# One summed tile for two: the weight sums of two heads over tile pairs in three attention blocks

## The chip, the core and the metric

The kernel runs on one core of one Trainium2 chip. The metric is device microseconds of one execution. The kernel before was run three times; each execution of it does the whole computation in one launch.

## What is computed

A graph attention layer over 4096 nodes of 256 features and 4 heads, and after it a mixture of 8 experts of which each node uses two.

```python
e = leaky_relu(s_row[:, :, None] + s_col[:, None, :], negative_slope=0.2)   # per head, 4096 x 4096
e = where(adj > 0, e, -9e15)
att = softmax(e, axis=-1)
out = einsum('hij,hjk->hik', att, h)          # then elu, + residual, layer norm, + x
...
top_w, top_i = top_k(xf @ Wg + bg, 2)          # softmax over the two
out = sum over e of w_dense[:, e] * (gelu(xf @ W1[e] + b1[e]) @ W2[e] + b2[e])
```

The softmax is not formed as such. For a neighbour `j` and a node `i` of one head the kernel holds a weight without the factor that belongs to `j` alone; that factor, exp(0.2 s_col), is multiplied into the features `ha` and stands by itself in `unit`. The sum over all `j` of weight times features goes to `acc`, and the sum over all `j` of weight times factor goes to `den`; the quotient of the two is the head's output.

## The kernel before

**Blocks and tiles.** The 4096 nodes `i` are cut into four blocks of 1024 (`a`, 0 to 3; the words block 1 to 4 are used for them). A block runs over 32 tiles `j` of 128 neighbours each. A tile has 128 neighbours on the partitions and 1024 nodes along the row, and each node row stands in two halves of 512. `attend` and `weigh` do one tile.

**One tile.** SyncE loads the adjacency of the tile. ScalarE turns it into a bfloat16 mask `am` of zeros and twos (`mask_of`, L1603; three buffers). VectorE makes one weight tile `w` of 128x1024 float32 for each of the four heads in the order 1, 0, 2, 3, each with one scalar_tensor_tensor: the maximum of the row term `er` and the neighbour's `eb`, and the minimum of that and the mask (L1686). The `w` tiles have ten buffers, two and a half tiles' worth, and this is how far VectorE can run ahead of TensorE. TensorE then multiplies: for each head and half two 128x32 matmuls into `acc` (`rows_of_head`, L1195) and one 128x2 matmul into `den` (`weights_of_head`, L1204). [...]A float32 matmul shows as two records in the trace, so a tile has 32 records of `acc` and 16 of `den`.

**The end of a block.** `finish_blocks(a)` is a generator. Its first step, taken when the block ends, copies `den` and `acc` to SBUF on ScalarE, so that the next block can use the banks. The other steps are taken one by one while the next block runs, one after each tile, by `next(pending, None)` in the tile loop. Step 1 turns `den` and forms its reciprocals (`shares_of`), steps 1 to 17 make the block's output rows (results, elu, residual, two layer norms, with three DMAs that add or store), steps 18 to 25 route the rows to experts (`route_rows`: transposes `ptx`, logits, top two, and at step 25 the ranks by the matmul `pk`, L1322 and L1324). Step 26 turns the ranks to places `at` (L1342), and 16 indirect DMAs on GpSimd's queue scatter the rows to the expert lists in DRAM (L1382).

**Order.** The order of TensorE's instructions is written out by hand inside the attention: `queue` and `order_of` chain every matmul and transpose in the order of the program text. The other engines are ordered by a planner at build time, which takes, of the instructions that it holds ready, the one that stands first in the text. Every engine then works its own list strictly in order. DMAs are issued from SyncE's, ScalarE's and GpSimd's lists.

**Behind the attention.** The expert phase works through jobs of 256 rows. `up` is the first product (L1867), `down` the second (L1901). The rows of job 1 on are loaded by `load_full` (L560, the tile `early`) after the attention, `ROOM` of them ahead of the first job. Within TensorE's written order `up` of job 0 comes first, then pieces of the last block's end, then the transposes of job 1's rows (`turn_rows_of`, L604), then `down` of job 0. The program keeps every read of the expert lists behind the scatters that stand before it in the text: the first `early` load waits for the semaphores of all 16 scatters of block 3. Jobs 0 to 8 (`EARLY` is 9) hold rows of the first two blocks alone; their places were planned in block 4.

[...]four for `acc`, one for `den`, and three that the helper `bank` gives out in turn.

Of the kernel before, what the change touches and what calls it, by code (L numbers as in the profile page):

```python
# [10 lines left out]
F32 = mybir.dt.float32  # L11
I32 = mybir.dt.int32
BF16 = mybir.dt.bfloat16
AF = mybir.ActivationFunctionType
OP = mybir.AluOpType
# [17 lines left out]
FINAL = (16, 15, 15, 15, 13, 13, 12, 9)  # L33
LIST = 36 * CH
PLACE = (2, 3, 0, 1)
ORDER = (1, 0, 2, 3)


# [6 lines left out]
def gat_then_moe(  # L45
# [34 lines left out]
    MID = BOTH - EARLY  # L80
    LATE = 2 * N // TT - BOTH
    SURE = 2
    ROOM = 10
    KT = -(-N // TT)
    LAG = 6

# [132 lines left out]
    def forward(apart, stack):  # L219
# [392 lines left out]
        with ExitStack() as layer:  # L612
# [588 lines left out]
            def weights_of_head(w, j, half, h):  # L1201
# [4 lines left out]
                    start=(j == 0 and half == 0), stop=(j == NT - 1 and half == HB - 1),  # L1206
                ))

            def attend(w, j, halves, sums_first=None):


                def first_heads():
                    for half in halves:
                        for h in (1, 0):
                            rows_of_head(w, j, half, h)

                def other_heads():
                    for half in halves:
                        for h in (1, 0):
                            weights_of_head(w, j, half, h)  # L1220
                        rows_of_head(w, j, half, 2)
                    for half in halves:
                        rows_of_head(w, j, half, 3)
                        for h in (3, 2):
                            weights_of_head(w, j, half, h)

                parts = (first_heads, other_heads)
                if sums_first is None:
                    sums_first = j in (0, NT - 1)
                for add in reversed(parts) if sums_first else parts:  # L1230
                    add()

            def shares_of(pd):

                z = small.tile([P, TB, H, HB], F32, tag="z", name="z")
                for h in range(0, H, 2):
                    nc.vector.reciprocal(z[:, :, h : h + 2], pd[:, :, PLACE[h] : PLACE[h] + 2, :HB])
                return z
# [151 lines left out]
            def finish_blocks(a):  # L1390
# [12 lines left out]
                for t in range(TB):  # L1403
                    order_of(nc.tensor.transpose(
                        pd[:, t].rearrange("p h q -> p (h q)"), ud[:, ts(t, P)], ident
                    ))
                z = shares_of(pd)
                xe = rows_listed()
                n = HB * TB
                halves = [(half, slice(half * TB, (half + 1) * TB)) for half in range(HB)]  # L1410
# [108 lines left out]
            def turn_sums(ud):  # L1519
                pd = bank([P, TB, H, Q], "pd")  # L1520
                for t in range(TB):
                    queue(nc.tensor.transpose(
                        pd[:, t].rearrange("p h q -> p (h q)"), ud[:, ts(t, P)], ident
                    ))
                z = shares_of(pd)
                return z

            def last_block(b, u, z, given, xe):

# [64 lines left out]
            def load_mask(a, j):  # L1594

                at = load_adj(gat, range(a * R, (a + 1) * R), j, 1, 3)
                am = gat.tile([P, R], BF16, tag="am", name="am", bufs=3)
                with tc.issue_after(marks["eb"]):
                    mask_of(at[:, 0], am)
                return am  # L1600
# [75 lines left out]
            else:  # L1676

                with tc.tile_pool(name="sep", bufs=2) as work:

                    def weigh(er, am, j, halves):  # L1680
# [10 lines left out]
                                w[half][h] = wh[:, half]  # L1691
                        return w

                    both = list(range(HB))
                    ers = [er0, er1]
                    er = er0
# [27 lines left out]
                        if j == 0:  # L1724
                            sums_turned(row)
                    for a in range(NR):
                        later = None
                        for j in range(0 if a else TB, NT):
                            attend(
                                weigh(er, load_mask(a, j), j, both), j, both,  # L1730
                                False if (a, j) == (NR - 1, NT - 1) else None,
                            )
                            if a == 0:
                                prepare_at(TB + j)
                            if pending:
                                next(pending, None)
                            if a == 1 and j == 1:
                                turn_biases()
                            if a + 1 == NR and j == 3:
# [366 lines left out]
```

## Time and profile before

| | us |
|---|---|
| median of three runs | 1264.79 |
| the three runs | 1264.42, 1264.79, 1270.94 |
| the profiled execution | 1259.9 |
| its span, first to last instruction | 1258.2 |
| busy in it: TensorE matmul, VectorE, ScalarE, GpSimd | 1243.7, 842.8, 451.6, 240.2 |
| mean granted TensorE clock | 0.997 |

The attention fills the first 778 us of the span and the expert phase the rest. On TensorE block 2 runs from 255.9 to 432.5 us, block 3 to 604.3 and block 4 to 778.3. Busy time is the time in which an engine had an instruction in work; what is said of waits comes from the semaphores. A line number in the profile is that of the listing above.

### The profile page before, as it was taken

The page shows a single profiled execution, that of the slowest core. Times are in us where ns is not written, and L with a number is a line of the kernel's source. Part 1 is how long each engine was busy: PE and PEld are TensorE (multiplying, and loading weights), DVE is VectorE, ACT ScalarE, POOL GpSimd, SP SyncE. Part 2 cuts the span into 40 slices and gives each one's busy share as a digit, 9 for nine tenths or more (in the row PEclk, how much of TensorE's full clock was granted, in tenths as well). Part 3 has the DMA queues.
Part 4 walks back from the last instruction along what each step waited for, and adds up shares of the span by engine and source line. Part 5 has one row for each costly group of instructions (what it writes and reads, how often), then busy time and mean ns, then how long its engine had stood idle before and what let it go on. Part 6 is the DMA issues. An engine that isn't in the chain of part 4 may idle for free.

```text
span 1258.2 us, 22490 instructions
## 1 busy us (share of the span) xinstructions
PE 1243.7 (99%) x8916; PEld 650.9 (52%) x8916; DVE 842.8 (67%) x1566; ACT 451.6 (36%) x929; POOL 240.2 (19%) x217
## 2 busy tenths in 40 slices
PE   9999999999999999999999999999999999999997
PEld 5444444332232332332325324888888876666686
DVE  7998887879999989999999996845111121111120
ACT  4332322255522375322655322533333332222322
POOL 4000000001002601006110024135222322122222
PEclk9999999999999999999999999999999999999999
DMA  6333433436533656335366423967777795454662
GB/s 215 118 119 124 158 105 102 166 102 133 187 105 104 231 118 201 103 100 158 112 167 194 119 80 108 329 184 225 234 208 222 207 210 115 102 139 105 139 156 42
DMA packets 131603, 190.22 MB, mean 151 GB/s; under 512 B 45560, under 2 KB 101744, under 8 KB 131104
## 3 DMA queue, kind: packets, MB, share of 16 engines
q1 hardware_dynamic: 109456, 145.39, 38.7%
q0 software_dynamic: 20544, 36.74, 13.2%
q10 hardware_dynamic: 1488, 6.55, 1.4%
q8 instruction: 72, 1.18, 0.4%
q14 instruction: 43, 0.35, 0.1%
HBM read 155.77 MB, written 29.74 MB: 147 GB/s over the span
## 4 chain that ended last, share of the span: by engine, by line
PE 94%; DVE 3%; issue 1%; DMA 1%; ACT 1%; POOLq 0%; SPq 0%; DVEq 0%; ACTq 0%
PE acc L1195 33%; PE po L1901 18%; PE ph L1867 17%; PE den L1204 17%; PE pr L1050 2%; DVE w L1686 2%; PE ph L1098 2%; PE pt L604 1%; PE ptx L1250 0%; DMA early<-lists 0%; PE acc L891 0%; PE pt L777 0%; PE ptr L1488 0%; PE po L1940 0%; PE pl L1261 0%
## 5 line engine op out<-in xcount | busy, mean ns | idle before, releaser
L1195 PE MATMUL acc<-w,ha 128*32 128x512 f32 x4096 | 671.6, 595 | 1.3 <-ACT u L1398 0.9
L1686 DVE SCALAR_TENSOR_TENSOR w<-er,eb,am 128x1024 f32<-128x1024 f32 x496 | 606.1, 1277 | 32.1 <-PE den L1204 31.8
L1204 PE MATMUL den<-w,unit 128*2 128x512 f32 x2048 | 467.8, 593 | 0.1
L1195 PEld LDWEIGHTS acc<-w,ha 128*32 128x32 f32 x4096 | 184.7, 110 | 294.3 <-issue 255.5
L1603 ACT ACTIVATE am<-adj 128x1024 bf16<-128x1024 int32 x124 | 130.6, 1054 | 348.8 <-DVE w L1686 208.9
L1867 PE MATMUL ph<-xT,w 128*128 128x256 f32 (+5 forms) x864 | 229.9, 423 | 0.2 <-ACT hT L1871 0.2
L1901 PE MATMUL po<-w,hT 128*128 128x256 f32 (+1 forms) x1040 | 229.7, 379 | 0.0
L1871 ACT ACTIVATE hT<-ph,bias 128x256 f32<-128x256 f32 (+5 forms) x216 | 111.3, 517 | 289.7 <-PE ph L1867 175.4
L1901 PEld LDWEIGHTS po<-w,hT 128*128 128x128 f32 (+1 forms) x1040 | 194.8, 189 | 30.7 <-issue 3.4
L1867 PEld LDWEIGHTS ph<-xT,w 128*128 128x128 f32 x864 | 163.4, 190 | 59.7 <-issue 38.0
L1204 PEld LDWEIGHTS den<-w,unit 128*2 128x2 f32 x2048 | 93.7, 85 | 148.2 <-issue 139.8
L1926 POOL DMA_INDIRECT out<-o,ids x66 | 102.0, 1546 | 323.7 <-DMA out<-o,ids 126.9
L1914 DVE SCALAR_TENSOR_TENSOR o<-po,share,b2s 128x256 f32<-128x256 f32 (+2 forms) x66 | 31.8, 483 | 196.4 <-PE po L1901 188.3
L1382 POOL DMA_INDIRECT lists<-xe,at x64 | 88.1, 1377 | 267.3 <-issue 184.3
L608 DVE COPY xT<-pt 128x256 f32<-128x256 f32 x12 | 5.1, 424 | 62.0 <-PE pt L604 54.1
L1851 DVE STREAM_TRANSPOSE xT<-xr 128x960 f32<-128x960 f32 (+5 forms) x10 | 10.0, 1004 | 31.6 <-PE ph L1867 31.1
L1050 PE MATMUL pr<-wr,xT 128*128 128x256 f32 x128 | 30.4, 381 | 0.2 <-ACT er L1144 0.2
L1889 ACT ACTIVATE b2s<-b2b,share 128x256 f32<-128x256 f32 x68 | 30.3, 503 | 0.0
L1438 POOL DMA_DIRECT2D xf<-in_x x6 | 8.1, 1351 | 105.4 <-ACT xf L1437 105.4
L1118 POOL DMA_DIRECT2D residual<-rb x6 | 4.7, 784 | 121.2 <-DVE rb L1065 121.2
L1050 PEld LDWEIGHTS pr<-wr,xT 128*128 128x128 f32 x128 | 24.1, 190 | 5.4 <-issue 0.9
L1098 PE MATMUL ph<-wall,xT 128*128 128x264 f32 x96 | 24.6, 399 | 0.0
(391 smaller groups left out, 658.5 us busy)
## 6 DMA issues: line engine op xcount, KB each, us to landing
adj<-in_adj SPq DMA_DIRECT2D x126, 512.0 KB
w<-in_L_ffn_W SPq DMA_DIRECT2D x54, 1024.0 KB
er<-parts ACTq DMA_DIRECT2D x3, 2048.0 KB
early<-lists SPq DMA_DIRECT2D x16, 260.0 KB
lists<-zeros POOLq DMA_DIRECT2D x8, 520.0 KB
residual<-rb POOLq DMA_DIRECT2D x8, 512.0 KB
rb<-residual SPq DMA_DIRECT2D x8, 512.0 KB
out<-y POOLq DMA_DIRECT2D x8, 512.0 KB
```

Of the source, the lines that this page charges most:

```text
L1050: order_of(nc.tensor.matmul(pr[:, k, :], turned[b][:, c, ts(t0 + k, P)], wr[:, c, :], start=(c == 0), stop=(c == DC - 1),))
L1098: order_of(nc.tensor.matmul(phs[t - t0], xT[:, c, ts(t, P)], wall[:, c, :], start=(c == 0), stop=(c == DC - 1),))
L1195: queue(nc.tensor.matmul(acc[half][h // 2][here : here + Q, :], ha[:, j, h * K + g * Q : h * K + (g + 1) * Q], w[half][h], start=(j == 0), ...
L1204: queue(nc.tensor.matmul(den[here : here + HB, :], unit[:, j, h, 1 - half : 1 - half + HB], w[half][h], start=(j == 0 and half == 0), stop ...
L1382: ins = nc.gpsimd.indirect_dma_start(lists, bass.IndirectOffsetOnAxis(ap=at[:, k, t : t + 1], axis=0), xe[:, t, :], None,).ins
L1603: nc.scalar.activation(am, at, AF.Relu, scale=2.0)
L1686: marks["w"] = nc.vector.scalar_tensor_tensor(wh[:, these], er[:, these, h], eb[:, j, h : h + 1], mask[:, these], op0=OP.max, op1=OP.min,).ins
L1867: order_of(nc.tensor.matmul(ph, job["w1"][:, c, ts(f, P)], xT[:, c, :], start=(c == 0), stop=(c == DC - 1),))
L1871: job["gelu"] = nc.scalar.activation(hT[:, f, :], ph, AF.Gelu, bias=job["bias"][:, f : f + 1]).ins
L1901: order_of(nc.tensor.matmul(po[:size], hT[:, f, k * CH : k * CH + size], w2[:, f, :], start=(f == 0), stop=(f == FC - 1),))
L1914: given_out.append(nc.vector.scalar_tensor_tensor(o[:size], po[:size], share[:size, k : k + 1], b2s[k][:size], op0=OP.mult, op1=OP.add,).ins)
L1926: added.append(add().ins)
```

## The change

In blocks 2 to 4 (`a` of 1 to 3) the tile loop takes other helpers.

- In the first 18 tiles (`PAIRED`) the mask is copied once more by ScalarE, as 512 words of 32 bits, into one of two PSUM banks (`packed_mask`), and VectorE's four instructions read it there. The banks are two of the three that `bank` gives out.
- For heads 1 and 0 these tiles go to `den` in pairs. When the second tile of a pair is weighed, ScalarE multiplies the first tile's weights by the quotient of the two tiles' factors (`ratio`, made once in block 2) into a slot of the `er` tile that is idle, GpSimd adds the second tile's weights in place (`added_pair`), and the next tile's `attend_both` multiplies the sum with the second tile's factors. So heads 1 and 0 have one set of `den` matmuls per pair in place of two; heads 2 and 3 and all `acc` matmuls stay. The rows of `den` get another order (`place_of`), which `shares_of` follows.
- The steps of `finish_blocks` are no more taken from the block's first tile on, one per tile: they are taken from tile 18 on, two per tile, and up to nine after the last tile.
- `ROOM`, the number of row tiles loaded ahead in the expert phase, goes from 10 to `EARLY - 1`, which is 8.

```diff
+PAIRED = 18
+ADDED = (1, 0)
...
-    ROOM = 10
+    ROOM = EARLY - 1
...
+            def attend_both(w, j, alone, summed=None, sums_first=False):
+                halves = range(HB)
+                def first_heads():
+                    for half in halves:
+                        for h in (1, 0):
+                            rows_of_head(w, j, half, h)
+                def other_heads():
+                    if summed:
+                        for h in ADDED:
+                            for half in halves:
+                                weights_by_half(summed, j - 1, half, h)
+                    if alone:
+                        for h in (1, 0):
+                            for half in halves:
+                                weights_by_half(w, j, half, h, start=(j == 0))
+                    for half in halves:
+                        for h in (2, 3):
+                            rows_of_head(w, j, half, h)
+                    for h in (2, 3):
+                        for half in halves:
+                            weights_by_half(
+                                w, j, half, h, start=(j == 0 and not alone), stop=(j == NT - 1)
+                            )
+                parts = (first_heads, other_heads)
+                for add in reversed(parts) if sums_first else parts:
+                    add()
...
+                    def packed_mask(am, j):
+                        pm = masks[j % 2]
+                        nc.scalar.copy(pm.bitcast(I32), am.bitcast(I32))
+                        return pm.bitcast(BF16)
...
+                    def added_pair(idle, j):
...
+                        for k, h in enumerate(ADDED):
+                            s = slots[:, 2 * (j // 2 % 2) + k]
+                            nc.scalar.activation(
+                                s, made[0][h], AF.Copy, scale=ratio[:, j // 2, h : h + 1]
+                            )
+                            nc.gpsimd.tensor_tensor(s, s, made[1][h], OP.add)
...
                         for j in range(0 if a else TB, NT):
-                            attend(
-                                weigh(er, load_mask(a, j), j, both), j, both,
-                                False if (a, j) == (NR - 1, NT - 1) else None,
-                            )
+                            if a == 0:
+                                attend(weigh(er, load_mask(a, j), j, both), j, both)
+                            else:
+                                w = weigh_both(er, a, j)
+                                attend_both(
+                                    w, j, j >= PAIRED, summed,
+                                    j == 0 or j == NT - 1 and a + 1 < NR,
+                                )
+                                summed = None
+                                if j < PAIRED and j % 2:
+                                    summed = added_pair(ers[(a + 1) % 2], j)
...
-                            if pending:
-                                next(pending, None)
+                            if pending and j >= PAIRED:
+                                for _ in range(2 if j + 1 < NT else 9):
+                                    next(pending, None)
```

## The prediction

> **What bounds the kernel now.** I read the engines' busy time, the costliest groups, the chain that ended last, the busy time by block, and the timelines of VectorE, GpSimd and SyncE about the block ends.
>
> ```profile
> PE 1243.7 (99%) x8916; PEld 650.9 (52%) x8916; DVE 842.8 (67%) x1566; ACT 451.6 (36%) x929; POOL 240.2 (19%) x217
> ...
> L1686 DVE SCALAR_TENSOR_TENSOR w<-er,eb,am 128x1024 f32<-128x1024 f32 x496 | 606.1, 1277 | 32.1 <-PE den L1204 31.8
> ```
>
> TensorE is busy in 99% of the span. VectorE's 32 us before its weights end on TensorE: its buffers were full. The chain, at the end of the attention, gives the price of a record, and the timeline of VectorE that of a weight instruction:
>
> ```profile
> 773.48 1.72 PE acc L1195 x16
> ```
> ```profile
> 403.35 6.06 DVE L1686 SCALAR_TENSOR_TENSOR w<-er,eb,am 128x1024 f32<-128x1024 f32 x5
> ```
>
> Sixteen records take 1.72 us, 107.5 ns each, so a tile's 48 take 5.16. Five weights take 6.06, the last 1.28 long, so they start 1.195 apart: 4.78 a tile. VectorE gains 0.38 us a tile, which pays for the rest of its work. By block:
>
> ```profile
> 255.90:432.50 176.60, 175.68 (x1635) 53.84 (x1638) 167.26 (x198) 75.52 (x153) 33.14 (x22) 0.99 0.47 137
> 432.50:604.30 171.80, 171.80 (x1623) 52.81 (x1619) 166.09 (x190) 74.06 (x151) 29.75 (x23) 1.00 0.49 142
> 604.30:778.30 174.00, 173.59 (x1623) 61.62 (x1615) 161.26 (x215) 70.91 (x149) 27.62 (x22) 1.00 0.43 124
> ```
>
> After the length come TensorE, weight loads, VectorE, ScalarE, GpSimd. VectorE stands at 94% of TensorE: a gain on TensorE beyond some 6 us a block would meet it.
>
> GpSimd does little, but late in block 4 this (64 scatters in all, starts 1.3 to 2.4 us apart):
>
> ```profile
> 746.94 1.28 POOL L1382 DMA_INDIRECT lists<-xe,at  x1 [81.76 <-DVE at L1342]
> 748.53 2.09 POOL L1382 DMA_INDIRECT lists<-xe,at  x1 [0.30 <-issue]
> ...
> 770.89 0.97 POOL L1382 DMA_INDIRECT lists<-xe,at  x1 [0.30 <-issue]
> 772.17 0.97 POOL L1382 DMA_INDIRECT lists<-xe,at  x1 [0.30 <-issue]
> ```
>
> They end 5 us before the attention does. Behind it the chain goes through the rows of job 1, and TensorE's timeline shows what they hold up:
>
> ```profile
> 780.59 5.91 DMA early<-lists
> ...
> 788.71 6.91 PE po L1901 x32
> ```
> ```profile
> 778.56 7.17 PE L1867 MATMUL ph<-xT,w 128*128 128x256 f32 x32
> ...
> 787.53 0.41 PE L604 MATMUL pt<-ident,early 128*128 128x128 f32 x2 [0.48 <-PE ptr L1536]
> ...
> 788.55 7.07 PE L1901 MATMUL po<-w,hT 128*128 128x256 f32 x32
> ```
>
> The load is issued 2.3 us after the last attention matmul (778.3) and lands 5.9 us later; the transposes of its rows (`pt`) wait, and `po` of job 0 comes behind them in TensorE's order.
>
> [...]a scatter, which reads its places in SBUF, takes 0.97 us after VectorE's last weight at 768.4 and often 2.0 to 2.1 before. [...]
>
> **The change, part by part.**
>
> *Matmuls.* A pair saves two heads times two halves, 8 records: 0.86 us. 9 pairs in 3 blocks: 27 x 0.86 = **-23.2**. All of it is on TensorE's path.
>
> *Masks in PSUM.* 18 x 4 x 3 = 216 weights read one input there. At 1.195 a paired tile takes VectorE 4.78, TensorE (18 x 5.16 - 7.7)/18 = 4.73: VectorE loses 0.9 us in 18 tiles, which its lead covers (9 us at block starts, from the starts of `w` and of the matmuls on them in the timeline). The price in PSUM is not shown for this form. [...]the 512-wide product from PSUM (L1539) takes 0.69 us, and the 1024-wide one in SBUF (L1446) 1.22, which less half of the weight form's width (1.278 - 0.743 = 0.535) is also 0.69. Nothing excludes a few ns less, but TensorE would cap that gain. I take **0**[...].
>
> *ScalarE.* A pair adds two mask copies and two scaled copies. [...]hidden by ScalarE's idle time, **0**. Without that cover the copy is late for the weight two tiles on.
>
> *GpSimd.* [...]The sum is wanted one tile after the second weight: **0** in the steady state. An add that takes 4.7 us or more would set the pace.
>
> *Steps at double pace.* VectorE's share of the first ten steps costs 12 us over its 4.78 a tile (block 3: tiles 2 to 9 took 50 us in the timeline). In five tiles in place of eight its lead falls from 9.5 by 12, and gets back 1.9 from the tiles and 2.7 from the transposes (tiles 0 and 1 of block 3 took 6.72 and 6.31 us): about 2 us stay. In block 4 before, a lead of 2 cost TensorE 0.9 us. DMAs of a step have half the time too: the accumulating one goes out at 306.3 and is waited for until 312.1, against 7.7 us for three steps. I take 1 a block, **+3**, ends 0 and +9. Block 4's early plan no longer meets these steps: **-1**.
>
> *Scatters at the block's end.* Step 25, the rank matmul, moves from tile 24 to tile 30, and TensorE's order keeps it behind that tile: 5.2 us before the block's end E. From it to the first scatter were 5.6 us (741.36 to 746.94). So 16 scatters start at about E+0.4, and all stand in GpSimd's list before the next block's adds if the planner holds them ready first, as I expect, since VectorE's lead is then some 4.5 us and the adds want the weights of tile 1. [...]they take 0.97 + 0.30: 20.3 us[...]. TensorE wants that sum in tile 2: two tiles of 4.3 and 1.7 of the third, E+10.3. It stands for 15 us, with VectorE behind it on full buffers. This meets blocks 3 and 4: **+30**. If the adds of the first pair come ahead, the second pair's are late: [...]8 each. Bounds 0 (finely mixed) and 17 each.
>
> *The load after block 4.* Its scatters, now at E-2 to E+0.6, take 20[...] to 26 us (as before): they end at E+18 to E+27[...]. The first `early` load waits for all of them, and SyncE's list stands behind it with job 1's weights. It was issued at E+2.3. TensorE has `up` of job 0 (7 us) and then the transposes of these rows, ahead of `down`. So everything after moves by 18 to 27 us; I take **+20**, lower end 15. `ROOM` moves loads 9 and 10 behind: these waited on the same scatters; **0**.
>
> Sum: -23.2 + 0 + 3 - 1 + 30 + 20 = **+28.8**. The profiled execution has 1259.9 us (1.7 outside its span of 1258.2) and would have 1289; it is 4.9 below the median of the runs, 1264.79, from which I forecast **1292 us**.
>
> **Rivals.**
> 1. *The adds come ahead of the scatters*: 8 in place of 15 a block, +15: 1280. For it: VectorE can lead by two tiles; against it: the steps eat that lead just before.
> 2. *Scatters and adds mix well, so only the late load is lost*: 0 to 3 a block, the load 20 to 27: -1 to +12, 1264 to 1277. [...]against it: all 16 become ready at one moment.
> 3. *Faster*: the scatters reach neither TensorE nor the load, because the route steps run early enough: -23 + 3 - 1, 1244; it decides if the last scatter lands before E+7 and the adds before E+10. Against it: the rank matmul is fixed behind tile 30, and 16 x 1.27 us follow.
> 4. *GpSimd locks VectorE out although the masks are in PSUM*: each add would hold a weight back[...]. Against it: [...]the scatters' spread.
> That the pairing does not take place at all I exclude: the matmuls are issued by number.
>
> **How the numbers follow.** The forecast 0.45, rival 1 0.22, rival 2 0.12, faster 0.13, the lock or another slow case 0.08. The runs tell about 0.5%, 6 us, from no change. Forecast and rival 1 are slower (0.67), with 4 and the upper half of rival 2 (0.02) 0.77; rival 2 leaves 0.10 to same; faster 0.13. The forecast's own range is 1280 to 1311 (waits of 12 to 17 us, load 15 to 27, steps 0 to 9: +15 to +46). With rivals 1 and 2 the range is 1260 to 1311, which leaves out rivals 3 and 4.
>
> **What would show it.** The `den` group at 1832 records in place of 2048; weights near 1.28 us with PSUM masks; [...]scatters beginning within 2 us of the ends of blocks 2, 3 and 4; a TensorE wait on GpSimd of 10 to 15 us early in blocks 3 and 4; the first `early` load issued some 20 us behind the attention. Wrong would be: block 2 not shorter than 172 us (matmul price), no wait on GpSimd (order), or `po` of job 0 within 12 us of the attention's end (load).

## The result, and the profile after

The changed kernel takes 1360.82 us (median of four runs, 1358.88 to 1361.47), the kernel before beside it 1265.17: a ratio of 1.0745, with a 95% interval of 1.0723 to 1.0766. The forecast was 1292, the range 1260 to 1311. The direction is right; the size, 95.7 us, is 3.3 times the predicted 28.8, and outside the range. The profiled execution took 1360.74 us, with a span of 1359.0, 100.8 more than that of before.

From the page of the changed kernel, the engines' busy time and the groups that answer to those shown of before (out and in, shape, count, then busy us, mean ns of one, idle us before it and its releaser):

```profile
PE 1260.4 (93%) x8700; PEld 657.4 (48%) x8700; DVE 857.8 (63%) x1570; ACT 538.7 (40%) x1037; POOL 344.1 (25%) x271
...
L1756 DVE SCALAR_TENSOR_TENSOR w<-er,eb,pm 128x1024 f32<-128x1024 f32 x216 | 259.4, 1272 | 16.3 <-POOL er L1775 11.3
...
L1756 DVE SCALAR_TENSOR_TENSOR w<-er,eb,am 128x1024 f32<-128x1024 f32 x168 | 210.4, 1294 | 41.4 <-PE den L1217 40.6
...
L1775 POOL TENSOR_TENSOR er<-er,w 128x1024 f32<-128x1024 f32 x54 | 127.4, 2382 | 143.6 <-DVE w L1756 127.4
...
L1300 PE MATMUL ptx<-ident,xe 128*128 128x128 f32 x64 | 13.6, 341 | 39.9 <-ACT xe L1528 39.7
```

TensorE was busy in 99% of the span and is now in 93% of a longer one: it does 216 records less and stands for some 99 us. VectorE's weights are no dearer with the mask in PSUM (1272 ns against 1294), and the adds take 2.38 us. New is the last line. These 64 transposes of the rows to be routed, which TensorE had never waited for, are waited for 39.7 us. The same group in the costliest groups of the kernel before:

```profile
L1250 PE MATMUL ptx<-ident,xe 128*128 128x128 f32 x64 | 8.6, 278 | 0.0
```

The prices of a record and of a weight are as before. In the changed kernel's chain of work that ended last, and in its timeline of VectorE:

```profile
481.04 3.00 PE acc L1197 x28
```
```profile
289.30 23.91 DVE L1756 SCALAR_TENSOR_TENSOR w<-er,eb,pm 128x1024 f32<-128x1024 f32 x20
```

28 records take 3.00 us, 107.1 ns each, and twenty weights, the last 1.27 long, start 1.19 us apart. The busy time by stretch, block 2, 3, 4 and what lies behind (start and end, length; then TensorE, weight loads, VectorE, ScalarE, GpSimd; then the granted clock, DMA share and GB/s):

```profile
260.10:457.40 197.30, 174.79 (x1562) 52.91 (x1562) 170.56 (x198) 105.71 (x190) 56.28 (x32) 0.92 0.42 123
457.40:652.10 194.70, 175.39 (x1543) 60.55 (x1545) 167.95 (x190) 101.20 (x184) 56.77 (x33) 0.94 0.43 128
652.10:860.90 208.80, 182.33 (x1552) 58.38 (x1547) 176.73 (x220) 97.77 (x182) 66.71 (x43) 0.93 0.36 104
860.90:1359.00 498.10, 474.81 (x2102) 375.43 (x2102) 124.30 (x547) 154.31 (x319) 142.84 (x109) 0.98 0.67 172
```

Blocks 2 to 4 took 176.6, 171.7 and 174.4 us before and take 197.3, 194.7 and 208.7. Block 2 begins 4.2 us later, and what lies behind the attention has grown from 479.6 to 498.1. So 78 us are in the blocks, 4 at the start of block 2 and 18.5 behind the attention.

To see where in a block, I took from the trace the start of each tile's first record on TensorE, and from the length of the tile its records at 107.4 ns (48 in a whole tile, 40, 48 or 56 in a paired or adjoining one). What is left, called the surplus of a tile below, is TensorE's other work and its waits, in us for blocks 2 to 4 together:

| tiles | 0-2 | 3-17 | 18-19 | 20-25 | 26-27 | 28-31 | sum |
|---|---|---|---|---|---|---|---|
| before | 12.1 | 4.9 | 6.1 | 2.8 | 1.0 | 0.9 | 27.8 |
| after | 28.3 | 8.9 | 21.8 | -0.1 | 59.5 | 10.6 | 129.0 |
| difference | +16.2 | +4.0 | +15.7 | -2.9 | +58.5 | +9.7 | +101.2 |

With the records saved (-23.2), the start of block 2 (+4.2) and the part behind (+18.5) that is 100.7, the whole of the 100.8. Of it 81 lie in tiles 18 to 31, where the moved steps are, and where no tile is paired. Of the 81, some 48 us are waits of TensorE for two sets of transposes that belong to these steps: 8.4 at `ptr` (steps 1 and 2, tile 18) and 39.7 at `ptx` (step 18, tile 26).

**Tile 26.** From the timeline of all engines about it in block 2 (start, duration, what; in brackets the idle time before, and its releaser):

```profile
396.85 1.22 DVE L1496 TENSOR_TENSOR y<-y,gam 128x1024 f32<-128x1024 f32 x1
...
398.37 0.85 POOL L1497 DMA_DIRECT2D y<-xf  x1 [1.45 <-DVE y L1496]
...
405.52 0.42 ACT L1503 ACTIVATE m<-y 128x256 f32<-128x256 f32 x1 [1.18 <-DMA y<-xf]
...
407.25 0.17 DVE L217 TENSOR_SCALAR off<-total 128x8 f32<-128x8 f32 x1 [3.20 <-ACT m L1503]
407.33 4.87 DVE L1756 SCALAR_TENSOR_TENSOR w<-er,eb,am 128x1024 f32<-128x1024 f32 x4
407.46 0.51 ACT L209 ACTIVATE m<-y,off 128x256 f32<-128x256 f32 x1 [0.24 <-DVE off L217]
...
414.73 1.28 DVE L1756 SCALAR_TENSOR_TENSOR w<-er,eb,am 128x1024 f32<-128x1024 f32 x1
...
416.32 0.17 DVE L1515 TENSOR_TENSOR off<-off,r 128x8 f32<-128x8 f32 x1
416.52 1.09 ACT L1528 ACTIVATE xe<-y,off,r 128x256 f32<-128x256 f32 x2 [1.96 <-DVE off L1515]
417.17 0.18 PEld L1300 LDWEIGHTS ptx<-ident,xe 128*128 128x128 f32 x1 [13.54 <-ACT xe L1528]
417.17 0.48 PE L1300 MATMUL ptx<-ident,xe 128*128 128x128 f32 x1 [12.61 <-ACT xe L1528]
```

This is one chain through four engines and a transfer: VectorE's product, GpSimd's accumulating transfer (7.2 us to landing), ScalarE's sums, VectorE's mean, ScalarE's squares, VectorE's roots, ScalarE's normalised rows, TensorE's transposes. From the product to the transposes it takes 20 us. But these are only the last of the steps, and the four tiles between their places in the text, 20.6 us, would just do; the product itself came late, in TensorE's tile 25, though it stands behind tile 22 in the text. What shows the stand is the whole chain between two of TensorE's own instructions, from the last `ptr` transposes to the first `ptx`. From TensorE's timeline of the changed kernel, and from the timelines of TensorE and ScalarE of the kernel before, in block 2:

```profile
360.59 1.12 PE L1538 MATMUL ptr<-ident,u 128*128 128x128 f32 x4 [0.55 <-ACT y L1543]
```
```profile
271.56 1.09 PE L1488 MATMUL ptr<-ident,u 128*128 128x128 f32 x8
...
337.85 4.04 ACT L1478 ACTIVATE xe<-y,off,r 128x256 f32<-128x256 f32 x8 [1.96 <-DVE off L1465]
...
355.32 1.09 PE L1250 MATMUL ptx<-ident,xe 128*128 128x128 f32 x8
```

Before, the first rows `xe` came 65 us behind the end of `ptr`, and TensorE, at one step a tile, reached `ptx` only after 83: it never waited. At two steps a tile only eight tiles stand between the two, 41 us of records, while the chain takes 55 (361.7 to 417.2). TensorE takes its list in order, and stands for most of the difference, 12.6 us.

TensorE doesn't wait for weights there; three of the next tile's four were made when it stopped. VectorE, though, is not far ahead and not at rest. It waits 3.2 us for ScalarE's sums, and makes seven more weights during the stand, three of them between the instructions of the roots. So its own weights are part of the chain's length.

This stand of TensorE, 12.6 us without work, costs more than its length. The same stretch by busy time, clock in the third column from the end:

```profile
404.60:409.00 4.40, 0.00 (x0) 0.00 (x0) 1.75 (x3) 3.25 (x15) 0.77 (x1) 1.00 0.95 300
409.00:417.10 8.10, 0.00 (x0) 0.00 (x0) 7.41 (x12) 5.18 (x16) 0.00 (x0) 0.51 0.75 250
417.10:421.00 3.90, 3.78 (x16) 1.88 (x20) 0.00 (x0) 3.90 (x10) 0.00 (x0) 0.50 0.22 84
421.00:424.00 3.00, 3.00 (x24) 0.64 (x20) 0.00 (x0) 0.51 (x2) 0.00 (x0) 0.70 0.00 0
```

TensorE's granted clock is 1.00 in the first 4.4 us of standing, 0.51 in the other 8.1, and still half for some 5.7 us after it has begun again (0.50 in the first 3.9, and by the mean of 0.70 some 1.8 of the last 3.0). Its first eight transposes take 2.80 us there, where the eight of tile 27 take 1.09, and the 16 records behind them 3.33, where the next 16 take 1.89: 3.2 us beside the 12.6. Tile 26 has 15.5 us beyond its records and tile 27 some 4.

**Behind the attention.** TensorE's and SyncE's timelines answer to the last lines shown of before:

```profile
868.21 1.13 PE L1971 MATMUL ph<-xT,w 128*128 128x256 f32 x4 [3.02 <-issue]
875.29 2.07 PE L1971 MATMUL ph<-xT,w 128*128 128x256 f32 x4 [5.96 <-issue]
880.97 3.78 PE L1971 MATMUL ph<-xT,w 128*128 128x256 f32 x8 [3.60 <-ACT hT L1975]
...
887.06 0.63 PE L606 MATMUL pt<-ident,early 128*128 128x128 f32 x4
887.52 7.07 PE L2005 MATMUL po<-w,hT 128*128 128x256 f32 x32
```
```profile
862.63 0.70 SPq L1897 DMA_DIRECT2D w<-in_L_ffn_W  x1
879.04 0.37 SPq L562 DMA_DIRECT2D early<-lists  x1
```

The first `early` load goes out 18.2 us behind the attention's end at 860.9, in place of some 2, as forecast. But TensorE doesn't stand at the transposes of its rows: it stands in `up` of job 0, between its own matmuls, while the scatters run (857.6 to 877.6), and at 887 the transposes don't wait. Two waits lie one under the other there, and the profile can't say what either would cost alone.

### The profile page after: what moved, and what is told of

It reads as the page before. It is cut to its first block, busy times and chain, and to the rows that moved or that the text cites. A ratio compares the mean times of both kernels' runs of the same rounds, so it can differ in the third digit from the quotient of the medians.

```text
span 1359.0 us, 22410 instructions
## 1 busy us (share of the span) xinstructions
PE 1260.4 (93%) x8700; PEld 657.4 (48%) x8700; DVE 857.8 (63%) x1570; ACT 538.7 (40%) x1037; POOL 344.1 (25%) x271
## 4 chain that ended last, share of the span: by engine, by line
PE 72%; DVE 11%; issue 9%; DMA 2%; ACT 2%; POOL 2%; another core or an unknown queue 1%; POOLq 0%; DVEq 0%; ACTq 0%
PE acc L1197 22%; PE po L2005 17%; PE ph L1971 16%; DVE w L1756 9%; PE den L1217 5%; PE den L1206 4%; PE pr L1052 2%; PE ph L1100 2%; DMA y<-xf 2%; POOL lists L1432 1%; PE ptx L1300 1%; POOL er L1775 1%; PE pt L606 1%; PE acc L893 0%
## 5 line engine op out<-in xcount | busy, mean ns | idle before, releaser
L1197 PE MATMUL acc<-w,ha 128*32 128x512 f32 x4096 | 585.1, 609 | 19.0 <-DVE w L1756 12.5
L1197 PEld LDWEIGHTS acc<-w,ha 128*32 128x32 f32 x4096 | 162.8, 112 | 323.3 <-issue 283.4
L1756 DVE SCALAR_TENSOR_TENSOR w<-er,eb,pm 128x1024 f32<-128x1024 f32 x216 | 259.4, 1272 | 16.3 <-POOL er L1775 11.3
L1971 PE MATMUL ph<-xT,w 128*128 128x256 f32 (+5 forms) x864 | 234.2, 428 | 14.4 <-issue 10.6
L1756 DVE SCALAR_TENSOR_TENSOR w<-er,eb,am 128x1024 f32<-128x1024 f32 x168 | 210.4, 1294 | 41.4 <-PE den L1217 40.6
L1217 PE MATMUL den<-w,unit 128*2 128x512 f32 x1104 | 173.0, 597 | 3.0 <-issue 2.8
L1775 POOL TENSOR_TENSOR er<-er,w 128x1024 f32<-128x1024 f32 x54 | 127.4, 2382 | 143.6 <-DVE w L1756 127.4
L1735 DVE SCALAR_TENSOR_TENSOR w<-er,eb,am 128x1024 f32<-128x1024 f32 x112 | 138.2, 1276 | 13.3 <-PE den L1206 13.3
L1206 PE MATMUL den<-w,unit 128*2 128x512 f32 x512 | 117.6, 592 | 0.1
L1432 POOL DMA_INDIRECT lists<-xe,at x64 | 62.5, 976 | 144.4 <-issue 58.7
L1746 ACT COPY pm<-am 128x512 int32<-128x512 int32 x54 | 31.8, 591 | 119.3 <-DVE w L1756 113.6
L1217 PEld LDWEIGHTS den<-w,unit 128*2 128x2 f32 x1104 | 35.2, 86 | 88.9 <-issue 87.7
L1772 ACT ACTIVATE er<-w,ratio 128x1024 f32<-128x1024 f32 x54 | 59.1, 1137 | 5.7 <-DVE lesse L289 3.0
L1300 PE MATMUL ptx<-ident,xe 128*128 128x128 f32 x64 | 13.6, 341 | 39.9 <-ACT xe L1528 39.7
```

The costliest lines, as they stand in the source:

```text
L1197: queue(nc.tensor.matmul(acc[half][h // 2][here : here + Q, :], ha[:, j, h * K + g * Q : h * K + (g + 1) * Q], w[half][h], start=(j == 0), ...
L1206: queue(nc.tensor.matmul(den[here : here + HB, :], unit[:, j, h, 1 - half : 1 - half + HB], w[half][h], start=(j == 0 and half == 0), stop ...
L1217: queue(nc.tensor.matmul(den[here : here + HB, :], unit[:, j, h, 1 - h // 2 : 1 - h // 2 + HB], w[half][h], start=start, stop=stop,))
L1432: ins = nc.gpsimd.indirect_dma_start(lists, bass.IndirectOffsetOnAxis(ap=at[:, k, t : t + 1], axis=0), xe[:, t, :], None,).ins
L1735: marks["w"] = nc.vector.scalar_tensor_tensor(wh[:, these], er[:, these, h], eb[:, j, h : h + 1], mask[:, these], op0=OP.max, op1=OP.min,).ins
L1756: marks["w"] = nc.vector.scalar_tensor_tensor(wh, er[:, :, h], eb[:, j, h : h + 1], mask.rearrange("p (s r) -> p s r", s=HB), op0=OP.max, ...
```

## The experiments

Each kernel was timed beside the kernel before on the same chip; "+" is against that one's median (1260 to 1266 us).

**1. The steps alone.** The kernel before with the steps from tile 18 on, two a tile, nine in the last, and the new `ROOM`; no pairs, no masks in PSUM, no adds.

```diff
-    ROOM = 10
+    ROOM = EARLY - 1
...
-                            if pending:
-                                next(pending, None)
+                            if pending and j >= 18:
+                                for _ in range(2 if j + 1 < NT else 9):
+                                    next(pending, None)
```

> The kernel before with only the block-end steps moved (from tile 18 on, two per tile, up to nine after the last) and ROOM at 8; no pairs, no PSUM masks, no GpSimd adds. Theory P (TensorE's written order waits for the steps: the chain from the turned sums to the normalised rows is longer than the eight tiles it now has): waits of TensorE of 5 to 8 us at tile 18 and 13 to 16 us at tile 26 of each block, and the late load behind block 4 (+18): 1265 + 3 x 20 + 18 = 1340 us. Theory G (GpSimd's adds and the paired tiles make the loss): only the late load and small losses, 1265 + 18 + 3 = 1286 us.

1344.95 us, +84.6, ratio 1.0673 (1.0615 to 1.0731). This is the first theory's 1340. The moved steps alone lose nine tenths of what the whole change loses net. (The new `ROOM` is in this run and in run 5 and was not run alone; run 6 keeps the old one.) Tile 26 takes 21.7, 21.6 and 22.0 us in the three blocks, as in the changed kernel.

**2. Pairs with the steps where they were.** The changed kernel with one step a tile from tile 0, and pairs and PSUM masks in tiles 4 to 17.

```diff
-                        mask = packed_mask(am, j) if j < PAIRED else am
+                        mask = packed_mask(am, j) if 4 <= j < 18 else am
...
-                            if pending and j >= PAIRED:
-                                for _ in range(2 if j + 1 < NT else 9):
-                                    next(pending, None)
+                            if pending:
+                                next(pending, None)
```

> The changed kernel with the steps back at one per tile from tile 0, and the pairs and PSUM masks in tiles 4 to 17 (the first four tiles keep three PSUM banks for the steps). Theory P: every long wait of TensorE goes, seven pairs save 3 x 7 x 0.86 = 18 us, and VectorE, with nothing to spare, gives part of it back where the steps' two-input instructions meet adds (up to 2.4 us each, some 12 a block): 1250 to 1290 us. Theory G: the adds are what costs, with seven ninths of them left the time stays above 1320 us.

1288.02, +27.6, ratio 1.0205 (1.0158 to 1.0253). The long waits and the late load are gone (480.6 us behind the attention). But the 21 pairs, which save 18.1 us of records, cost more: tiles 3 to 17 have 46.4 us beyond their records, where the kernel before has 4.9. VectorE's steps meet the adds there. One group of them, from the costliest groups of the run (an instruction of the roots, done six times):

```profile
L163 DVE TENSOR_TENSOR q<-r 128x8 f32<-128x8 f32 x6 | 8.7, 1455 | 0.0
```

In the kernel before, the same instruction takes 0.16 us. This group and four more of the steps' (the products with `gam`, the sums with `rb`, and two of the roots) take 24 us more than before, which is over half of the 41.5.

**3. Without the adds.** The changed kernel without GpSimd's add, so the second tile's weights of heads 1 and 0 are left out of the denominators.

```diff
-                            nc.gpsimd.tensor_tensor(s, s, made[1][h], OP.add)
```

> The changed kernel without the 54 GpSimd adds: the sum is left at the first tile's scaled weights, so the second tile's weights of heads 1 and 0 are missing from the denominators. Theory P: the waits for the sums behind the scatters (7.7 us in block 3, 15 us in block 4) and VectorE's wait behind adds in the early plan (about 10 us) go, the waits at tiles 18 and 26 stay: 1325 to 1340 us. Theory G: below 1300 us.

1399.9, ratio 1.1091 (1.1038 to 1.1143), which misses the expectation, in the first place for a reason beside the question: with other denominators the rows go to other experts, the expert phase does more work (32 matmuls more in each of its two products), and what lies behind the attention takes 552 us in place of 498. Only the attention can be compared. It ends at 847.6, 13.3 us earlier, where the expectation saw 21 to 36. In tiles 0 to 2, where the prediction saw TensorE standing for the late sums, the surplus is 24.8 us against 28.3. Tiles 1 and 2 of block 4 take 24.3 us without any add, and 24.7 with.

So the sums add only 3.5 us in three blocks, but not because they are in time. From the changed kernel's timelines of GpSimd and TensorE, the first two adds of block 4 and the first matmuls on their sums:

```profile
672.41 4.67 POOL L1775 TENSOR_TENSOR er<-er,w 128x1024 f32<-128x1024 f32 x2
```
```profile
676.79 1.08 PE L1217 MATMUL den<-er,unit 128*2 128x512 f32 x2
```

Both sums are ready at 677.1, 25.0 us behind the end of block 3, and the prediction has them wanted 10.3 us behind it. TensorE would have stood for them for some 14 us (an estimate from these times), but it gets to them late itself: something else has held it already. The two waits lie one under the other. This run shows what the other makes without the sums, 15.0 us in block 4; what the sums would make without the other was not run.

**4. The early plan out of the adds' way.** The changed kernel with block 4's plan and first tile behind tile 19 in place of 3.

```diff
-                            if a + 1 == NR and j == 3:
+                            if a + 1 == NR and j == 19:
```

> The changed kernel with the early plan and its first load at tile 19 of block 4 in place of tile 3. Theory L (the plan's small two-input VectorE instructions are held up by GpSimd's adds, as one of 3.46 us where the kernel before has 0.15): block 4 falls by 8 to 14 us, to about 1350 us. Rival: the plan is only slow because VectorE's queue was full there, and the loss moves with it: 1358 to 1362 us.

1348.65, ratio 1.0689 (1.0636 to 1.0743); block 4 falls from 208.7 to 198.9. So the plan costs 9.8 us where it stands. Its first instruction in the timeline of VectorE, of the changed kernel and of the kernel before:

```profile
678.30 3.46 DVE L360 TENSOR_TENSOR ne<-filled,starts 128x8 f32<-128x8 f32 x1
```
```profile
617.05 0.16 DVE L358 TENSOR_TENSOR ne<-filled,starts 128x8 f32<-128x8 f32 x1
```

Eight elements a partition, held for 3.3 us, with the weights of the next tiles behind them. The instruction ends as the second of two adds in a row does (677.0 to 679.4 and 679.4 to 681.7).

**5 and 6. Pace against place.** Run 1 moves the steps late and doubles their pace. These two take each alone: the kernel before with the steps from tile 6 on, one a tile, nine in the last, so that they end in the same tiles as in run 1, and the new `ROOM`; and with two a tile from tile 0.

```diff
+                            if pending and j >= 6:
+                                for _ in range(1 if j + 1 < NT else 9):
+                                    next(pending, None)
```

> The kernel before with its steps from tile 6 on, one a tile, nine in the last; no pairs, no masks in PSUM, no adds. Beside the run with the steps alone from tile 18 (1344.95) only the pace differs, the last steps stand in the same tiles. Theory W (double pace): attention as long as before, the load some 18 us late: 1275 to 1285. Theory Q (lateness): about 1345, or at least 1320.

```diff
-                                next(pending, None)
+                                for _ in range(2 if j + 1 < NT else 9):
+                                    next(pending, None)
```

> The kernel before with two steps a tile from tile 0 on; they are over by tile 17, so scatters and load are earlier than before. With the steps alone from tile 18 at two a tile (+84.6 us) and those from tile 6 at one a tile (+26.3) it makes a table of pace against place. Theory W (the pace by itself): 58 us as there, or somewhat less since VectorE leads by 10 us at a block's start, so 1300 to 1325. Theory B (pace hurts only together with a late place, where the block's end leaves no room): 1265 to 1275.

Late at one a tile: 1291.3, +26.3, ratio 1.0193 (1.0167 to 1.0219), 6 us above its expectation. Early at two a tile: 1335.64, +75.7, ratio 1.0607 (1.059 to 1.0625), more than its expectation. So:

| | one step a tile | two a tile |
|---|---|---|
| early (tile 0 on) | 0 | +75.7 |
| late | +26.3 | +84.6 |

Of the lateness, what lies behind the attention makes 17.5 us by the profile of that run; the pace costs 58 us when late and 76 when early. TensorE's timeline of the early, doubled run has the same stand, 18 tiles sooner:

```profile
524.55 2.80 PE L1250 MATMUL ptx<-ident,xe 128*128 128x128 f32 x8 [13.55 <-ACT xe L1478]
```

**7. Six paired tiles.** The changed kernel with `PAIRED` at 6 and one step a tile.

```diff
-PAIRED = 18
+PAIRED = 6
...
-                                for _ in range(2 if j + 1 < NT else 9):
+                                for _ in range(1 if j + 1 < NT else 9):
```

> The changed kernel with 6 paired tiles a block in place of 18, and the steps from tile 6 on one a tile (nine in the last), so that they end at the same tile as in the changed kernel. Theory W (the double pace makes the waits at the transposes of `z` and of the route's rows): these waits go, the load behind block 4 stays some 18 us late, pairs gain 9 x 0.86 = 7.7: 1260.4 - 7.7 + 18, and up to 10 of small waits, 1271 to 1285. Theory Q (it is the lateness of the steps, their place before the block's end): the waits stay and with them 15 to 25 us a block, 1320 or more.

1307.99, +43.0, ratio 1.0332 (1.0315 to 1.035). Tiles 18, 26 and 27 are down to their work, as the pace says (11.2 us beyond their records in tiles 18 to 27, against 81.2 in the changed kernel), but the time is 18 us above the top of the expectation, counted from its own kernel before (+43.0 against +24.6). Tiles 0 to 2 keep 28.1 us, as in the changed kernel: something at the block's start is neither pace nor, by run 3, the sums alone.

**8. What holds the block's start.** The 16 scatters of block 2's rows are moved behind the adds of tile 7 in block 4; those of block 1's rows stay ahead of block 3's adds. (The edit, of which this is a part, writes both sets behind tile 8; on GpSimd the planner puts the first one where it was.)

```diff
+                if b in (0, HB):
+                    held.append(scatter)
+                else:
+                    scatter()
...
+                            if j == 8 and held:
+                                held.pop()()
```

> The changed kernel with the 16 scatters of block 2's rows behind the adds of tile 7 in block 4's list of GpSimd; in block 3 they stay ahead of the adds. In the changed kernel TensorE takes 24.7 us for tiles 1 and 2 of block 4, where two tiles of such a kind need 9.4, and 24.3 without the adds too. Theory S (the scatters, or their transfers, hold TensorE): tiles 1 and 2 of block 4 fall to 9.4 to 11, tile 1 of block 3 stays at 12, and the 15 us come back in part where the scatters now are, at tiles 8 to 11, with the sums behind them late: 1348 to 1365 in all. Theory R (it is something else at the block's start, such as its banks or loads): tiles 1 and 2 stay at 23 to 25, and tiles 8 to 11 cost more on top: 1365 to 1380.

1357.67, ratio 1.0766 (1.0725 to 1.0807): no gain, but the loss has moved as expected of the scatters. Tiles 0 to 2 of block 4 fall from 15.4 us beyond their records to 0.1, tiles 3 to 17 rise from 9.0 to 24.1, of it 13.4 in tile 9. Block 3 is as it was. In the changed kernel, from the timeline of all engines in tiles 1 and 2 of block 4:

```profile
663.77 0.97 POOL L1432 DMA_INDIRECT lists<-xe,at  x1 [0.30 <-issue]
664.42 0.59 PE L1217 MATMUL den<-w,unit 128*2 128x512 f32 x1 [1.09 <-issue]
665.04 0.97 POOL L1432 DMA_INDIRECT lists<-xe,at  x1 [0.30 <-issue]
665.85 1.32 PE L1217 MATMUL den<-w,unit 128*2 128x512 f32 x2 [0.84 <-issue]
```

and in this run, in tile 9:

```profile
714.22 0.97 POOL L1436 DMA_INDIRECT lists<-xe,at  x1 [0.30 <-issue]
714.44 1.30 PE L1197 MATMUL acc<-w,ha 128*32 128x512 f32 x2 [1.50 <-issue]
715.50 0.97 POOL L1436 DMA_INDIRECT lists<-xe,at  x1 [0.30 <-issue]
716.54 1.86 PE L1197 MATMUL acc<-w,ha 128*32 128x512 f32 x2 [0.80 <-issue]
```

TensorE goes forward one or two records at a time, with gaps of up to 1.5 us that no semaphore explains, wherever these 16 scatters stand: from 8.7 us after the first of them in the changed kernel, from 8.5 in this run. In block 3 they come only 17 us after the first. The gaps depend on how close the scatters follow each other, but these runs give no rule. With 1.27 to 1.31 us between scatters in the mean, 6 to 15 us are lost. With 1.43 to 1.66 (blocks 3 and 4 of runs 1 and 5) there are small gaps, of 0.1 to 0.4 us, and some 3 to 6 us are lost. With 1.68 and more, in the kernel before, there is no gap. What lies between a scatter and TensorE wasn't tried. It isn't a late transfer of instructions: none is in the trace of the changed kernel from 654.5 to 680, and the gaps end at 674.3.

**9. Masks in SBUF.** The changed kernel without the copy of the mask.

```diff
-                        mask = packed_mask(am, j) if j < PAIRED else am
+                        mask = am
```

> The changed kernel with its masks in SBUF throughout (no copy of masks, no banks for them), so every weight reads two inputs in SBUF while GpSimd adds. Theory N (an add of two SBUF inputs doesn't hold VectorE's two-input instructions by more than it does the changed kernel's): 1350 to 1361, up to 10 less because the first weight of a block no longer waits for a bank. Theory X (each add holds a weight back for most of its 2.38 us): a pair takes VectorE 9.55 + 4.8 = 14.3 us against TensorE's 9.5, 4.8 more in each of 27 pairs, up to 130: 1430 to 1490, with weights in the first 18 tiles of clearly over 1.3 us.

1449.73, +184.7, ratio 1.1454 (1.1435 to 1.1473). From its page:

```profile
L1756 DVE SCALAR_TENSOR_TENSOR w<-er,eb,am 128x1024 f32<-128x1024 f32 x384 | 565.7, 1527 | 71.9 <-PE den L1217 55.6
...
L1775 POOL TENSOR_TENSOR er<-er,w 128x1024 f32<-128x1024 f32 x54 | 174.2, 3247 | 246.6 <-DVE w L1756 152.7
```

A weight now takes 1527 ns in the mean, where those with the mask in PSUM took 1272 in the changed kernel, and an add 3247 in place of 2382: both are longer. Tiles 3 to 17 have 104.3 us beyond their records, against 8.9. That is 95 us over the 22.5 pairs in these tiles, 4.2 us a pair, somewhat less than two adds of the changed kernel (2 x 2.38). The time is within the second theory's range. It is what the masks in PSUM save.

**10 and 11. Fewer pairs.** The steps as before, one a tile from tile 0, with pairs and PSUM masks in tiles 10 to 17 alone; and in tiles 18 to 25 alone, for which the next block's rows are loaded at tile 26.

```diff
+                        mask = packed_mask(am, j) if 10 <= j < 18 else am
```

> The changed kernel with its steps where they were before (one a tile from tile 0) and the pairs and PSUM masks in tiles 10 to 17 of each block alone. Theory W: no step waits, the load is not late, 12 pairs gain 10.3 us and lose up to 6 to what of VectorE's steps meets the adds: 1250 to 1258. Theory X (VectorE's two-input steps held by the adds cost more than the pairs save, as it was with pairs in tiles 4 to 17, +27.6): 12 pairs of 21 lose 12/21 of that, about 1262 to 1278.

```diff
+                        mask = packed_mask(am, j) if 18 <= j < 26 else am
...
-                            if j == 20 and a + 1 < NR:
+                            if j == 26 and a + 1 < NR:
```

> The changed kernel with its steps where they were before (one a tile from tile 0), pairs and PSUM masks in tiles 18 to 25 alone, and the next block's rows loaded at tile 26 in place of 20, since they go into the buffer of the sums. Theory V (a pair is worth its 0.86 us only where VectorE has a lead to give, and in tiles 18 to 25 of the kernel before that lead is 6 to 10 us and grows): 12 pairs, -10.3, of which up to 4 are lost: 1255 to 1260 beside 1265. Theory X (the adds hold VectorE's steps wherever they stand, or the later load of rows is waited for): 1266 to 1285.

Tiles 10 to 17: median 1271.51 of 20 runs that spread from 1266.0 to 1283.6, ratio 1.0044 (1.0028 to 1.0061), within half a per cent of no change. Its profiled execution is the slowest of the twenty, so only its block 3 is read, which takes 172.6 us against 171.7. Tiles 18 to 25: 1276.48, ratio 1.0134 (1.0117 to 1.0151), 1.3% slower, where 1255 to 1260 was expected of a VectorE with a lead to give. The lead of 6 to 10 us falls to 1.3 at tile 19, but not because VectorE is too slow: it waits up to 7.8 us for the copy of the mask, which stands in ScalarE's list behind copies that wait for TensorE. Tiles 18 and 19 grow by 1.9 us each or more. So in neither place do twelve pairs give back their 10.3 us, and no version that was run is faster than the kernel before.

**12. Room for the chain.** Run 6 with four empty steps between the accumulating transfer and the steps that read `y`, and four between the normalised rows and their transposes.

```diff
-                yield
+                for _ in range(5):
+                    yield
...
+                for _ in range(4):
+                    yield
                 yield from route_rows(a * HB, xe)
```

> As the run with two steps a tile from tile 0 (1335.64 beside 1259.95), but with four empty steps (two tiles) put between the transfer that adds `xf` to `y` and the steps that read `y`, and four between the normalised rows `xe` and their transposes. No work is taken away. Theory C (the chain from that transfer to the transposes has a length of its own, and TensorE, which takes its list in order, stands at the transposes when they are placed before its end): the surplus of tiles 8 and 9, 93.5 - 6 x 5.15 = 62.6 us in the three blocks, goes, all but some 20: 1273 to 1295. Theory D (twice as much VectorE and ScalarE work a tile is the cost, wherever the transposes stand): 1315 to 1340.

1320.77, +55.2, ratio 1.0427 (1.0389 to 1.0465): 20.5 us less than run 6, where 40 to 60 was expected of the chain, and within the other theory's 1315 to 1340. Tiles 8 and 9, where run 6 loses 62.6 us, take 5.15 and about 7 us: that stand is gone. But tile 13 now takes 12.7 in blocks 2 and 3, and in block 2 tiles 16 to 20 lose again. The next part of TensorE's own steps, the 16 transposes and the products on them, takes the wait over: in TensorE's timeline of this run

```profile
551.08 1.14 PE L1261 MATMUL pl<-xT,wg 128*32 128x128 f32 x16 [3.55 <-ACT xT L1253]
```

So the chain before the transposes is the largest stand, but not the whole price of the pace. The timeline reads as if two steps a tile leave each of TensorE's steps too close behind the one that feeds it. That isn't shown apart from the other theory, since VectorE's weights stand within the chain and twice the work a tile makes it longer.

## Why the prediction was wrong in size

By its own steps, in its order (its sum of 28.8 on 1264.79 gives 1293.6, not 1292, which changes nothing; and by its own lines VectorE stands at 95, 97 and 93% of TensorE in blocks 2 to 4):

- **Matmuls, -23.2**: right. 1104 + 216 `den` records in blocks 2 to 4 in place of 1536, at 107.1 ns.
- **Masks in PSUM, 0**: right in the steady state, 1272 ns. (The product L1539 that it took at 0.69 us has a median of 0.67.) Not seen was the start of block 2, 4.2 us later. The first mask is copied there only behind ScalarE's copy of `den`, the first weight is made only behind `hbar`, which waits for TensorE, and TensorE waits 4.0 us for the weights. That the shared banks cause it isn't shown: run 9, without these copies and banks, starts block 2 at 262.9, later still.
- **ScalarE, 0** and **GpSimd, 0** in the steady state: right. The copies of the mask take 0.59 us and the scaled ones 1.14, and the adds 2.38, below the 4.7 from which they set the pace; paired tiles 3 to 17 of blocks 2 and 3 have nothing beyond their records. What it reckoned with for these three lengths was the author's estimate; no trace of before showed them. Beside the adds, weights with the mask in PSUM take 1272 ns and with it in SBUF 1527 in the mean (run 9).
- **Steps at double pace, +3: the step that failed.** It counted VectorE's work against its lead, and of the steps' transfers only that they have half the time. It did not follow the whole chain of these steps from TensorE's `ptr` to its `ptx`, through four engines and the transfers, and set it against the eight tiles, 41 us, that half the spacing leaves. In the kernel before, that chain took 65 us, at a pace that is part of it; in the changed kernel it takes 55. What it mis-sized is TensorE's wait at its own steps: tiles 18 to 31 have 81 us more beyond their records. Runs 1, 5 and 6 show that the pace by itself costs 58 to 76 us, where the upper bound was 9. VectorE's lead, the thing reckoned with, does go down, to less than one tile when TensorE stops behind tile 26's records; but it is the rows `xe` that TensorE waits for there, not weights.
- **Early plan, -1**: wrong in sign, +9.8 beside the same plan at tile 19 (run 4). It left out that adds stand in the same tiles now: the plan's first instruction took 3.46 us beside two of them, in place of 0.16.
- **Scatters at the block's end, +30**: half the size, and only half the mechanism. The scatters begin at the ends of the blocks, or up to 10 us ahead, and stand before the adds; in block 4 the sums are ready 25.0 us behind the block's start, about where the forecast has them (wanted at 10.3, and 15 of standing), though for the length of an add it had only the author's estimate. But TensorE isn't there to wait for them: it is held in single records while the scatters run close together, which the prediction doesn't have. Tiles 0 to 2 lose 16 us more than before. In block 4 the hold alone makes 15.0 of 15.4 us (run 3) and goes where the scatters go (run 8); in block 3 it wasn't moved. The two waits lie one under the other.
- **The load after block 4, +20**: the size is right, 18.5, and so is the issue, 18.2 us behind the attention. Where TensorE stands is not as told: in `up` of job 0, so that the size is in part luck.

The sum as measured is -23.2 + 81 + 16.2 + 4.0 (9.0 in block 4, where the plan is, less the 4.9 of these tiles before) + 4.2 + 18.5 = 100.7. The first and second rivals fall with the order on GpSimd: in blocks 3 and 4 all 16 scatters stand ahead of the block's adds. The third, faster, falls on the late load, and on the pace that it left out as well. What the fourth supposes was not seen with the masks in PSUM; with them in SBUF (run 9) tiles 3 to 17 lose 4.2 us a pair.

## What to carry to other kernels

When steps are packed closer on an in-order engine, follow the longest chain between two of that engine's own instructions through every queue and transfer, and compare its length with the time that the new spacing leaves (here 55 us and 41). The busy time of the engine that seems short does not show it. Work of VectorE that had come into the time of GpSimd's adds cost up to 3.3 us an instruction here, more than one add of 2.38 (`ne`, with two inputs of eight elements a partition: 3.46 us in place of 0.16). And a saving on the bound engine has to be looked for in what feeds it: twelve pairs were worth nothing in either place, though in one VectorE had a lead to give, because the copies of the mask came late.

## What the hardware did that was not expected

- TensorE did not run freely beside scatters that GpSimd issued some 1.3 us apart: it went forward one or two records at a time, 6 to 15 us lost for 16 scatters. No semaphore explains it, but the loss moved with the scatters: tiles 0 to 2 of block 4 fell from 15.4 us to 0.1, tiles 3 to 17 rose from 9.0 to 24.1 (run 8).
- With the masks in PSUM the scatters went faster: 1.3 us apart in blocks 3 and 4, where run 9, with the masks back in SBUF, has 1.6 to 1.7. Over all 64 a scatter took 976 ns in the mean in the changed kernel, 1151 in run 9 and 1377 before.
- Behind a stand of 12.6 us TensorE worked at a granted clock of 0.50 for some 5.7 us, and took 3.2 us more for eight transposes and 16 records.
- An instruction of 8 elements a partition took 3.46 us beside two adds, in place of 0.16.
